# Which side of a raw page's round trip through memory is cut in four, and how many partitions each transfer spans

## The chip, the cores and the metric

The kernel runs on one core of a Trainium2 chip. The metric is the device time of one execution in microseconds (us). Engines are named as the profile names them: PE (TensorE), DVE (VectorE), ACT (ScalarE), POOL (GpSimd) and SP (SyncE). SP does no arithmetic here; its queue issues nearly all transfers, which 16 DMA engines then carry out.

## The reference

One transformer block with adaptive normalization, in float32, for `x` of 8 x 1024 x 512 and a condition of 8 x 512:

```
mod = silu(cond) @ Wada + bada            # six vectors of 512 for each sequence
sh_a, sc_a, gt_a, sh_m, sc_m, gt_m = split(mod, 6)
xm = layernorm(x, g1, be1) * (1 + sc_a) + sh_a
q, k, v = split(xm @ Wqkv, 3)             # 16 heads of 32
att = softmax(causal(q k^T / sqrt(32))) v
x = x + gt_a * (att @ Wproj + bproj)
xm = layernorm(x, g2, be2) * (1 + sc_m) + sh_m
x = x + gt_m * (gelu(xm @ W1 + b1) @ W2 + b2)   # hidden size 2048
```

## The kernel before, in words

The 8 sequences of 1024 tokens are cut into 16 blocks of 512 tokens. Each block goes through the normalization, the three projections, attention, the output projection and the two layers of the hidden part. The large products are done in Strassen's form, seven products of quarters in place of eight, with sums of weight quarters kept in memory. All weights pass through a ring of eight tiles `w` of 256 KB each (L358 to L362), fetched by SP in the order in which PE uses them; a tile is fetched anew when PE has used up the one in its place.

The order of all instructions on each engine is fixed when the program is built. A planner in the kernel keeps an estimated time for each engine and, for each buffer, when it is written and left (`now`, `written`, `left`; `note`, `note_pe`, `note_dma`). It chooses at each step the thread of work whose needs are due first. On the chip nothing is reordered: an engine that comes to an instruction whose operand is not there waits. In the built program each transfer of SP also waits for the landing of the transfer eight before it, since eight landing semaphores are used in turn.

Three places in it send data out to device memory and back, in order to change what lies in a partition.

The first is attention by rows. Six of the blocks (4, 6, 8, 10, 12 and 14) are attended "by rows": the scores of a unit have queries in partitions (`rows_unit`, L2017), ACT takes their exponential into a page `rows_p` of 128 x 2048 (L2036) and DVE transposes it in blocks of 32 x 32 (L2047). What is still to be moved are whole blocks between partitions. `spread_unit` does this by memory: it writes the page into `image` (L2060), gives its slot back, and later reads `image` into another page `turned` (L2076), from which PE forms the weighted values `po` (L2092). There are three page slots, and ten units in each of the six blocks, 60 in all. A read needs both the landed image and a free slot, and a slot becomes free when PE has used the page in it.

The second is the turn of normalized rows (`turn`): for 20 of the normalized tiles (14 for attention, 6 for the hidden part) the transposition is done by DVE in blocks (L714), one write of 1 MB into `held` (L723) and four reads into the tile `hat` (L728). DVE or ACT then apply gain and shift (L782, L788). The other tiles are transposed by PE (`by_pe`, L778).

The third is the load of `x` for the same 14 tiles of attention (`load_x`, L412): its token order in partitions has to be the one that the turn expects, so it is read in four transfers.

Q is 32 (`P // NTT`), NTT is 4, hd is 32, TB and D are 512. A transfer of 256 KB has 128 rows of 2 KB; as built before, each of the four `image` writes, `held` reads and `x` reads of one tile touches 32 partitions and has four rows for each of them.

Of the kernel before, what the change touches and what calls it, by code (L numbers as in the profile page):

```python
# [9 lines left out]
F32 = mybir.dt.float32  # L10
# [12 lines left out]
def kernel(  # L23
# [33 lines left out]
    nc = tc.nc  # L57
    B, T, D = x.shape
    HD = W1.shape[1]
    P = 128  # L60
    hd = D // H
    scale = float(hd) ** -0.5
    TB = 512
    NTT = TB // P
# [18 lines left out]
    kept = ctx.enter_context(tc.tile_pool(name="kept", bufs=1, space=bass.MemoryType.DRAM))  # L83
# [21 lines left out]
    def due(reads=(), writes=()):  # L105
        t = 0.0
        for k in reads:
            t = max(t, written.get(k, 0.0))
        for k in writes:
            t = max(t, left.get(k, 0.0))  # L110
        return t

    def note(engine, ns, reads=(), writes=(), port=False):
        start = max(now[engine], due(reads, writes))
        if port:
            start = max([start] + [b for a, b in pool_spans if a <= start < b])
        end = start + ns
        now[engine] = end
        if engine == "POOL":
            pool_spans.append((start, end))  # L120
            del pool_spans[:-16]
        for k in reads:
            left[k] = max(left.get(k, 0.0), end + SYNC)
        for k in writes:
            written[k] = end + SYNC
        return end

    def note_dma(ns, reads=(), writes=(), after=0.0):

        begun = max(now["SP"], due(reads, ()), after)  # L130
        now["SP"] = begun + ISSUE
        now["DMA"] = max(begun + BEGIN, now["DMA"]) + ns
        for k in writes:
            written[k] = now["DMA"] + LAND

    def note_pe(ns, form, reads=(), writes=()):
        now["PE"] = max(now["PE"], due(reads, writes))
        if shape[0] != form:
            shape[0] = form
            now["PE"] += SWITCH  # L140
        note("PE", ns, reads)
        spent[0] += ns
        for k in writes:
            written[k] = now["PE"] + PIPE
# [98 lines left out]
    def mlp_steps(n):  # L243
        return [("u", n, i) for i in range(NQ)] + [("d", n, part) for part in range(4)]
# [9 lines left out]
    for w in range(1, NB):  # L254
        n = w - 1
        m = mlp_steps(n)
# [29 lines left out]
    n = NB - 1  # L286
# [102 lines left out]
    rows = tmp.tile([P, TB], F32, tag="y", name="rows")[:n_rows, :P]  # L389
# [8 lines left out]
    Q = P // NTT  # L398

    def hat_tile(key):  # L400
        return tmp.tile([P, NTT, D], F32, tag="hat", name=f"hat_{key}", bufs=1)

    def load_x(n):
        b, h = blocks[n]
        rows = hat_tile(f"a{n}")
        written["hat free"] = NEVER
        for t in range(NTT):
            some = x[b, h * TB + t * P : h * TB + (t + 1) * P, :]
            if f"a{n}" in by_pe:
                nc.sync.dma_start(rows[:, t, :], some)  # L410
            else:
                nc.sync.dma_start(rows[ts(t, Q), :, :], some.rearrange("(t i) d -> i t d", i=Q))  # L412
            note_dma(3600, [], [("x", f"a{n}")])
        return rows

    x_pre = {0: load_x(0)}
    fetch()

# [134 lines left out]
    def add_job(job, reads, first=False):  # L553

        at = sum(1 for other in jobs if other[2]) if first else len(jobs)
        jobs.insert(at, (job, reads, first))
# [149 lines left out]
    def turn(key, rows, xm):  # L706

        small_blocks = xm.rearrange("p c n -> p (c n)")
        by_tile = small_blocks.rearrange("p (m h t i) -> p h m t i", m=NTT, h=NC, t=NTT)
        written["blocks", key] = NEVER  # L710

        def turn_tile(t):
            into = by_tile[:, :, :, t, :]
            nc.vector.transpose(into, rows[:, t, :].rearrange("p (h m i) -> p h m i", m=NTT, i=Q))  # L714
            done = [("blocks", key)] if t == NTT - 1 else []
            note("DVE", 620, [("hat", key, t)], done)

        for t in range(NTT):
            add_job(lambda t=t: turn_tile(t), [("hat", key, t)], key[0] == "m")
        yield [("blocks", key)], []  # L720
        held = kept.tile([P, NTT * D], F32, tag=f"held_{turns[0] % 2}", name=f"held_{key}")
        turns[0] += 1
        nc.sync.dma_start(held, small_blocks)  # L723
        note_dma(2600, [("blocks", key)], [("held", key)])
        yield [("held", key)], []
        for m in range(NTT):
            some = held[:, ts(m, D)].rearrange("(a i) d -> i a d", i=Q)
            nc.sync.dma_start(rows[ts(m, Q), :, :], some)  # L728
            note_dma(1250, [("held", key)], [("turned", key)])
        yield [("turned", key)], []  # L730

# [3 lines left out]
    def modulated(key, gain, shift, b, guards):  # L735
# [23 lines left out]
        if turned:  # L759
            yield from turn(key, got, xm)  # L760
# [590 lines left out]
    def perform(step):  # L1351
# [7 lines left out]
        elif kind == "columns_m":  # L1359
            columns_of["m"] = norm_columns("m", 3, 4, O_G2, O_BE2)  # L1360
        elif kind == "load_xa":
            x_pre[step[1]] = load_x(step[1])
        elif kind == "load_xr":
            start(load_xr(step[1]))
# [319 lines left out]
    def take_slot():  # L1684
        slot = free_p.pop(0)
        count_slots()
        return slot

    def give_slot(slot):
        free_p.append(slot)  # L1690
        count_slots()
# [362 lines left out]
    def spread_unit(n, raw, slot, parts, i):  # L2054

        yield [("p", slot)], []
        image = kept.tile([P, NTT, TB], F32, tag=f"image_{i % 5}", name=f"image_{n}_{i}")
        for a in range(NTT):
            into = image[:, a, :].rearrange("(b x) r -> x b r", x=hd)
            nc.sync.dma_start(into, raw[ts(a, hd)].rearrange("x (b r) -> x b r", b=NTT))  # L2060
            note_dma(700, [("p", slot)], [("image", n, i)])
        left["p", slot] = now["DMA"] + LAND
        written["image", n, i] += 1500
        raws.remove(slot)
        give_slot(slot)
        while True:
            yield [("image", n, i), SLOT, ("paged", n, i - 1)], []
            if free_p and len(pages) < 9:
                break
        taken_slot = take_slot()  # L2070
        pages.append(taken_slot)
        key = ("p", taken_slot)
        yield [], [key]
        written["paged", n, i] = 0.0
        page = pp.tile([P, NTT, TB], F32, tag=f"p{taken_slot}", name=f"turned_{n}_{i}")
        nc.sync.dma_start(page, image)  # L2076
        note_dma(2700, [("image", n, i)], [key])
        written[key] += 2000
        if i:
            yield [("valued rows", n, i - 1)], []  # L2080
        for qt, kh, c0, w, gg in parts:
            first = (n, gg) not in row_outs
            for k in range(w // P):
                yield [key, ("v", n), ("v done", n)], ["po"] if first and k == 0 else []
                if first and k == 0:
                    row_outs[n, gg] = [ps_po.tile([P, TB], F32, tag="o", name=f"po_{n}_{gg}"), 0]
                out = row_outs[n, gg]
                out[1] += 1
                for j in range(HPG):
                    r = slice(j * hd, (j + 1) * hd)  # L2090
                    at = c0 + k * P + j * hd
                    nc.tensor.matmul(  # L2092
                        out[0][r, ts(qt, P)],
                        vs[n][:, k, gg * P + j * hd : gg * P + (j + 1) * hd],
                        page[:, :, at : at + hd],
                        start=out[1] == 1,
                        stop=out[1] == 10,
                        skip_group_check=True,
                    )
                note_pe(2 * COLUMN * P, "columns", [key], ["po"])  # L2100
            if out[1] == 10:
                finish_rows(n, gg, out[0])
        pages.remove(taken_slot)
        give_slot(taken_slot)
        written["valued rows", n, i] = 0.0
# [27 lines left out]
    def finish_rows(n, g, out):  # L2133

        into = qTs[n][:, g, :]
        if wait_of(([("inverses", n, g)], [])) > 0 or max(now["DVE"], due(["po"])) > max(now["ACT"], due(["po"])) + 2500:
            nc.scalar.copy(into, out)
            note_act(585, None, ["po"], [("values", n, g)])
            start(scaled(n, g, into))
        else:  # L2140
            nc.vector.tensor_tensor(into, out, inverse_rows.pop((n, g)), ALU.mult)
            note("DVE", 690, ["po", "top"], [("att", n)])
            finished(n, g)
# [112 lines left out]
```

## Time and profile before

| | |
|---|---|
| median of 3 runs | 3537.45 us (3532.73 to 3537.84) |
| the profiled execution | 3537.05 us, span 3535.2 us |
| mean granted clock of TensorE | 0.988 |
| PE busy | 3398.7 us (96%) |
| DVE, ACT, POOL busy | 2287.1, 1249.8, 1790.1 us |
| moved | 610.88 MB, mean 173 GB/s |

The span is the time from the first to the last instruction of one profiled execution. A DMA queue's share is the time of its packets as a share of the span of all 16 DMA engines. In the rows of the profile a transfer is named by its tiles, as `turned<-image`, and SP's part of it, the issue, stands as SPq. TensorE works on float32 in two passes, so one matmul instruction has two records, and four matmuls of 32 columns run side by side.

### The profile page before, as it was taken

The numbers are of one execution on the slowest core, as the hardware profiler recorded it, in microseconds if no ns is written. First come the engines' busy times: TensorE is split into PE (matmuls) and PEld (weight loads), VectorE is DVE, ScalarE is ACT, GpSimd is POOL, SyncE is SP. The second block draws the span as 40 slices with busy tenths as digits, with TensorE's granted clock in tenths as the row PEclk, the third lists the DMA queues.
The fourth block names the chain that finished last, engine by engine and source line by source line (L and its number), as shares of the span: only waits on it lengthen the run. The fifth ranks groups of instructions, "written<-read, shape, count | busy, mean of one in ns | idle before, by whom it ended". The sixth has DMA issues, their size and how long they took to land.

```text
span 3535.2 us, 120275 instructions
## 1 busy us (share of the span) xinstructions
PE 3398.7 (96%) x53949; PEld 1726.5 (49%) x53949; DVE 2287.1 (65%) x2508; ACT 1249.8 (35%) x1878; POOL 1790.1 (51%) x1792
## 2 busy tenths in 40 slices
PE   8999999998999989999999999999999999999999
PEld 4444445454554545544454444544545445454455
DVE  5766675656667566675766657666667666576563
ACT  2334333252243522335323352323523334232421
POOL 3666846556038650476505764056730666308640
PEclk9999999999999999999999999999999999999999
DMA  6843434546755477553875548755487444863344
GB/s 199 262 149 112 139 94 137 149 113 209 231 187 155 115 236 222 182 152 109 262 234 166 146 116 266 235 159 145 134 280 219 140 141 159 276 200 110 96 134 140
DMA packets 373319, 610.88 MB, mean 173 GB/s; under 512 B 34748, under 2 KB 185084, under 8 KB 362308
## 3 DMA queue, kind: packets, MB, share of 16 engines
q1 hardware_dynamic: 372688, 603.15, 55.7%
q8 instruction: 425, 6.96, 0.8%
q14 instruction: 90, 0.74, 0.1%
q10 hardware_dynamic: 116, 0.03, 0.0%
HBM read 488.49 MB, written 112.46 MB: 170 GB/s over the span
## 4 chain that ended last, share of the span: by engine, by line
PE 78%; DVE 8%; DMA 6%; POOL 5%; issue 2%; SPq 1%; ACT 1%; ACTq 0%; DVEq 0%; POOLq 0%
PE bank L217 55%; PE sc L1613 6%; PE po L1760 5%; PE st L1719 5%; DMA turned<-image 3%; POOL pT L1854 3%; PE st L1707 2%; DVE mx L1628 2%; PE po L2092 2%; PE rows_sc L2017 1%; PE bank L1781 1%; DMA w<-in_L_cond_Wproj_dram 1%; DVE rows_max L2028 1%; DVE hT L167 1%; DVE sc L1625 1%
## 5 line engine op out<-in xcount | busy, mean ns | idle before, releaser
L1854 POOL TENSOR_TENSOR pT<-pT,pT 128x512 f32<-128x512 f32 (+3 forms) x966 | 1008.6, 1079 | 279.6 <-ACT pT L1732 230.1
L217 PE MATMUL bank<-w,hT 128*32 128x256 f32 x14336 | 824.3, 381 | 3.7 <-DVE hT L1226 2.9
L1732 ACT ACTIVATE pT<-st 128x2048 f32<-128x2048 f32 x228 | 428.3, 1879 | 749.5 <-PE st L1719 587.3
L1628 DVE TENSOR_REDUCE mx<-sc 128x4 f32<-128x2048 f32 (+3 forms) x287 | 522.8, 1839 | 243.0 <-PE sc L1613 239.6
L217 PEld LDWEIGHTS bank<-w,hT 128*32 128x32 f32 x14336 | 454.9, 110 | 388.0 <-issue 106.7
L217 PE MATMUL bank<-xm_m,w 128*32 128x256 f32 x8192 | 499.7, 381 | 0.0
L217 PE MATMUL bank<-t_m,w 128*32 128x256 f32 x6144 | 382.0, 380 | 8.2 <-DVE hT L208 8.2
L217 PEld LDWEIGHTS bank<-xm_m,w 128*32 128x32 f32 x8192 | 255.7, 110 | 218.5 <-issue 55.4
L2036 ACT ACTIVATE rows_p<-rows_sc,rows_minus 128x512 f32<-128x512 f32 (+3 forms) x384 | 196.8, 535 | 407.1 <-DVE rows_minus L2030 280.9
L217 PEld LDWEIGHTS bank<-t_m,w 128*32 128x32 f32 x6144 | 190.4, 110 | 181.9 <-issue 50.0
L1613 PE MATMUL sc<-kT,qT 32*128 32x512 f32 (+3 forms) x2296 | 262.1, 541 | 4.1 <-DVE mx L1628 2.4
L217 PE MATMUL bank<-w,qT 128*32 128x512 f32 x2048 | 245.1, 613 | 20.4 <-DMA w<-in_L_cond_Wproj_dram 19.5
L217 PE MATMUL bank<-xm_a,w 128*32 128x256 f32 x3968 | 245.8, 384 | 4.9 <-DVE u_q L208 2.2
L1760 PE MATMUL po<-pT,v 128*32 128x512 f32 (+3 forms) x2280 | 240.9, 513 | 7.1 <-POOL pT L1737 6.8
L1719 PE MATMUL st<-qT,kT 32*128 32x512 f32 (+3 forms) x2304 | 239.3, 505 | 0.0
L208 DVE TENSOR_TENSOR hT<-bank,u_u 128x512 f32<-128x512 f32 x183 | 122.7, 682 | 110.2 <-PE bank L217 102.5
L1737 POOL TENSOR_SCALAR_AFFINE_SELECT pT<-pT 128x512 f32<-128x512 f32 x160 | 117.9, 754 | 139.8 <-ACT pT L1732 139.8
L655 POOL TENSOR_SCALAR rstd_a<-mv_a 128x4 f32<-128x4 f32 x14 | 3.2, 230 | 363.2 <-DVE mv_a L634 362.8
L1625 DVE TENSOR_TENSOR sc<-sc,mask 128x1024 f32<-128x1024 f32 (+1 forms) x99 | 100.5, 1016 | 132.9 <-PE sc L1613 74.2
L217 PE MATMUL bank<-t_a,w 128*32 128x256 f32 x2944 | 185.3, 382 | 0.0
L217 PEld LDWEIGHTS bank<-xm_a,w 128*32 128x32 f32 x3968 | 127.6, 111 | 104.3 <-issue 23.0
L1129 ACT ACTIVATE hT<-hT,cols 128x512 f32<-128x512 f32 x256 | 164.8, 712 | 32.9 <-DVE hT L208 18.1
(270 smaller groups left out, 4149.7 us busy)
## 6 DMA issues: line engine op xcount, KB each, us to landing
w<-in_L_cond_W_dram SPq DMA_DIRECT2D x384, 256.0 KB
w<-kept_up_S SPq DMA_DIRECT2D x256, 256.0 KB
w<-kept_down_S SPq DMA_DIRECT2D x256, 256.0 KB
image<-rows_p SPq DMA_DIRECT2D x240, 256.0 KB
turned<-image SPq DMA_DIRECT2D x60, 1024.0 KB
w<-kept_qkv_S SPq DMA_DIRECT2D x180, 256.0 KB
w<-in_L_cond_Wqkv_dram SPq DMA_DIRECT2D x147, 256.0 KB
hat_a<-in_x_dram SPq DMA_DIRECT2D x64, 256.0 KB
```

The source lines that it names most:

```text
L208: nc.vector.tensor_tensor(out, src, other, op)
L217: nc.tensor.matmul(ps[r, :], columns, rhs, start=start, stop=stop, skip_group_check=True)
L1129: nc.scalar.activation(hT[:, i, :], hT[:, i, :], AF.Gelu, bias=cols[:, O_B1 + f : O_B1 + f + 1])
L1613: nc.tensor.matmul(sc[:, j, c0 : c0 + w], qTs[n][r, gg, ts(qt, P)], keys_of(n, kh)[r, gg, :w], start=True, stop=True, skip_group_check=True,)
L1625: nc.vector.tensor_tensor(place, place, shape_of.to_broadcast(place.shape), ALU.add)
L1628: nc.vector.tensor_reduce(maxima[n, gg][:, kh, qt, :], sc[:, :, c0 : c0 + w], axis=AX.X, op=ALU.max)
L1719: nc.tensor.matmul(st[:, j, c0 : c0 + w], kT[r, gg, ts(k % NTT, P)], qT[r, gg, TB - w :], start=False, stop=True, skip_group_check=True,)
L1732: nc.scalar.activation(pT[:, :, :used], st[:, :, :used], AF.Exp, scale=scale)
L1737: nc.gpsimd.affine_select(diagonal, diagonal, pattern=[[0, HPG], [1, P]], compare_op=ALU.is_ge, fill=0.0, base=0, channel_multiplier=-1,)
L1760: nc.tensor.matmul(po[r, TB - w :], v[:, k % NTT, g * P + j * hd : g * P + (j + 1) * hd], pT[:, j, c0 : c0 + w], start=(k == 0), stop=last ...
L1854: nc.gpsimd.tensor_tensor(into, into, pT[:, j, c0 : c0 + w], ALU.add)
L2036: nc.scalar.activation(tile_of[:, j], sc[:, j, c0 : c0 + w].rearrange("p (k b x) -> p k b x", b=NTT, x=hd), AF.Exp, bias=minus[:, i, j : j ...
```

## The change

For a unit's page the sides are exchanged: it is written by one transfer from all 128 partitions as it lies (8 KB rows), and read by four transfers, each of which fills one quarter of the length of all 128 partitions (2 KB rows). The reads of `held` and of `x` are still four for a tile, but each fills one quarter of all 128 partitions instead of the whole of 32. The bytes moved and the number of transfers stay as they are (1 + 4 in place of 4 + 1 for a unit). The planner's entries change with it: 2600 for the write in place of four times 700, and four times 690 for the read in place of 2700.

```diff
 load_x
-            some = x[b, h * TB + t * P : h * TB + (t + 1) * P, :]
             if f"a{n}" in by_pe:
-                nc.sync.dma_start(rows[:, t, :], some)
+                nc.sync.dma_start(rows[:, t, :], x[b, h * TB + t * P : h * TB + (t + 1) * P, :])
             else:
-                nc.sync.dma_start(rows[ts(t, Q), :, :], some.rearrange("(t i) d -> i t d", i=Q))
+                some = x[b, h * TB : (h + 1) * TB, :].rearrange("(m a i) d -> a m i d", a=NTT, i=Q)
+                nc.sync.dma_start(rows[:, t, :], some[t])
...
 turn
-        for m in range(NTT):
-            some = held[:, ts(m, D)].rearrange("(a i) d -> i a d", i=Q)
-            nc.sync.dma_start(rows[ts(m, Q), :, :], some)
+        for a in range(NTT):
+            some = held[ts(a, Q), :].rearrange("i (m d) -> m i d", m=NTT)
+            nc.sync.dma_start(rows[:, a, :], some)
             note_dma(1250, [("held", key)], [("turned", key)])
...
 spread_unit
-        image = kept.tile([P, NTT, TB], F32, tag=f"image_{i % 5}", name=f"image_{n}_{i}")
-        for a in range(NTT):
-            into = image[:, a, :].rearrange("(b x) r -> x b r", x=hd)
-            nc.sync.dma_start(into, raw[ts(a, hd)].rearrange("x (b r) -> x b r", b=NTT))
-            note_dma(700, [("p", slot)], [("image", n, i)])
+        image = kept.tile([P, NTT * TB], F32, tag=f"image_{i % 5}", name=f"image_{n}_{i}")
+        nc.sync.dma_start(image, raw)
+        note_dma(2600, [("p", slot)], [("image", n, i)])
...
-        nc.sync.dma_start(page, image)
-        note_dma(2700, [("image", n, i)], [key])
+        for a in range(NTT):
+            nc.sync.dma_start(page[:, a, :], image[ts(a, hd)].rearrange("x (b r) -> b x r", b=NTT))
+            note_dma(690, [("image", n, i)], [key])
```

## The prediction

> **What bounds the kernel now.** I read the page first: the parts on busy time, on the DMA queues and on the chain that ended last.
>
> ```profile
> span 3535.2 us, 120275 instructions
> PE 3398.7 (96%) x53949; PEld 1726.5 (49%) x53949; DVE 2287.1 (65%) x2508; ACT 1249.8 (35%) x1878; POOL 1790.1 (51%) x1792
> q1 hardware_dynamic: 372688, 603.15, 55.7%
> PE 78%; DVE 8%; DMA 6%; POOL 5%; issue 2%; SPq 1%; ACT 1%; ACTq 0%; DVEq 0%; POOLq 0%
> ```
>
> TensorE (PE) is busy for all but 3535.2 - 3398.7 = 137 us, so the change removes no work of the bounding engine; it can only alter how long PE waits. The DMA engines are busy 56% on average, but the kernel is uneven. So I asked next for the busy time of the six stretches in which a block is attended by rows, which is where the 60 raw pages go out to memory and come back. The first and the last of the six:
>
> ```profile
> core 0: us, PE busy (x) PEld busy (x) DVE busy (x) ACT busy (x) POOL busy (x), PEclk, DMA share, GB/s
> 833.00:1028.00 195.00, 176.28 (x2937) 96.04 (x2933) 134.56 (x160) 66.10 (x167) 33.01 (x34) 0.95 0.77 238
> 2977.00:3178.00 201.00, 191.56 (x3324) 106.97 (x3317) 140.64 (x158) 60.43 (x160) 46.52 (x37) 0.99 0.80 249
> ```
>
> In these 200 us stretches the DMA engines are already 0.77 to 0.80 busy, and PE idles 9 to 19 us in each. What PE waits for there stands in the list of waits (us in total, times, longest), and the chain shows one such wait in the fifth stretch (start, us, what).
>
> ```profile
> PEld po L2092 <- DMA turned<-image: 49.9, 19, 8.4
> PE po L2092 <- DMA turned<-image: 40.9, 18, 7.9
> ```
>
> ```profile
> 2613.03 1.05 PE po L2092 x32
> 2614.09 0.02 issue
> 2614.11 5.76 DMA turned<-image
> 2619.86 0.04 issue
> 2619.91 1.94 PE po L2092 x32
> ```
>
> When PE has used a page up, its slot is free, SyncE issues the next read into it at 2614.11, and PE stands still until it lands 5.8 us later. PE's order is fixed, so nothing is put in the gap. 19 + 18 = 37 waits on 60 reads: for most pages the read has no slack at all. A microsecond more per read is a microsecond more of time there.
>
> **How a transfer spreads.** The change keeps bytes and row lengths (8 KB rows one way, 2 KB the other) and changes which side is cut and how many partitions a transfer spans. I looked for moments in which one transfer ran nearly alone. First a 256 KB weight fetch into 128 partitions (317 to 318.7 us), then a 1 MB write of `held` from 128 partitions (1073.3 to 1077), a unit's writes from 32 partitions (3121 to 3127), and the 8 KB transfer of `inverse_rows` (883.9 to 885.2).
>
> ```profile
> DMA packets 144, 0.26 MB, mean 154 GB/s; under 512 B 16, under 2 KB 16, under 8 KB 144
> q1 hardware_dynamic: 144, 0.26, 42.4%
> ...
> DMA packets 144, 1.05 MB, mean 283 GB/s; under 512 B 16, under 2 KB 16, under 8 KB 16
> q1 hardware_dynamic: 144, 1.05, 69.1%
> ...
> DMA packets 681, 1.23 MB, mean 205 GB/s; under 512 B 80, under 2 KB 80, under 8 KB 681
> q1 hardware_dynamic: 681, 1.23, 93.3%
> ...
> DMA  0000000000000000000001222222000000000009
> DMA packets 69, 0.02 MB, mean 13 GB/s; under 512 B 68, under 2 KB 68, under 8 KB 68
> ```
>
> The first two have 128 data packets and 16 tiny ones, one with which each of the 16 DMA engines ends its part. The last has 64 packets of data (4 x 16 rows of 128 B) and only 4 tiny ones (the 69th packet is the next transfer's), and while it runs a fifth to a quarter of the DMA engines are busy (digit 2): its outermost dimension is 4, and 4 engines carried it. Costs in time of one engine: the weight fetch 0.424 x 16 x 1.7 us = 11.5 us, so 0.72 us on 16 engines or 2.9 us on 4. `held`: 0.691 x 16 x 3.7 = 40.9, 2.6 us on each of 16. The writes from 32 partitions: 0.933 x 16 x 6.0 = 89.6 us for 1.23 MB, which for 1.05 MB is 4.8 us on each of 16. So 32 partitions cost nearly twice what 128 do.
>
> The changed kernel's reads have, on the memory side, the list 4 x 32 x 512 (column block outermost), and on the SBUF side 128 x 512. No row of before mixes 4 and 128. The bounds are 4 engines and 16; I take 4, by the one row that has a 4 outermost. The Trainium skill, "DMA: Bandwidth & Descriptors", section on why a DMA increments its semaphore by 16, says that a transfer uses the largest number up to 16 that divides the slowest dimension of both sides; for 4 and 128 that is 4. The trace agrees for 4 with 4 (4 ending packets); for 4 with 128 no run here shows it.
>
> **The change part by part.** Durations are of the profiled execution, 3537.05 us around a span of 3535.2, which the median of the runs (3537.45) matches.
>
> Page reads (60, now four transfers each). One engine's part goes from 2.6 us (8 KB rows, taken from `held`) to 4 x 2.9 = 11.5 us: +8.9 us to landing. At the 37 waits nothing hides it: 329 us. The other 23 pages arrive before PE wants them, by how much differs: between 0 and 8.9 each; I take the middle, 102 us. What is late next is all that PE does behind `po`.
>
> Raw-page writes (60, now one transfer each): 4.8 to 2.6 us, -2.2. It counts where the read goes out as soon as the write lands:
>
> ```profile
> SPq L2076 <- DMA image<-rows_p: 9.9, 11, 1.8
> SPq L360 <- DMA turned<-image: 11.0, 5, 3.2
> ```
>
> 11 times: -24 us. Elsewhere the read waits for a slot and the gain is covered.
>
> SyncE's own time:
>
> ```profile
> L2060 SPq DMA_DIRECT2D image<-rows_p x240: 303/588/2450, 837.9 to 3157.4; - x120
> L2076 SPq DMA_DIRECT2D turned<-image x60: 319/374/1193, 846.7 to 3166.8; - x60
> L728 SPq DMA_DIRECT2D hat_a<-held_a x56: 302/430/1352, 137.1 to 3025.6; - x56
> ```
>
> 4 x 0.59 + 0.37 = 2.7 us per unit become 0.37 + 4 x 0.43 = 2.1 us. Nothing. Queued behind the reads on SyncE are the weight fetches.
>
> Normalized rows (20 turns of four reads): 4.8 us (32 partitions) become 11.5, +6.7. Who waited:
>
> ```profile
>   DVE xm_a L782: 10.6, 4
>   ACT xm_a L788: 9.1, 5
>   DVE xm_m L782: 2.9, 2
> ```
>
> 11 waits, of VectorE and ScalarE, not of PE. Behind them stand the evictions that free PE's three banks, so part of it comes through: between 0 and 20 x 6.7 = 134; I take half of 11 x 6.7, 37 us.
>
> Reads of `x` (14 blocks of four): nobody waits for them in the trace, they are early. But with the 20 turns they make 34 bursts that hold four engines 11.5 us instead of 4.8, and each weight fetch needs those four engines too. The cover is the ring of eight weight tiles:
>
> ```profile
> 2656.99 15.65 PE bank L217 x283
> PEld bank L217 <- DMA w<-in_L_cond_Wproj_dram: 24.8, 9, 6.4
> ```
>
> 283 records in 15.65 us are 55 ns each; a tile feeds 32 records, 1.8 us, and seven tiles in hand cover 12 us. That just hides a burst. Bounds 0 and 34 x 6.7 = 228; near the lower, 1 us each: 34 us.
>
> Waiting instructions of PE: as built, 969 instead of 866, since a page has four landings to wait for. At the one duration that the trace has for them, 103 x 0.051 = 5 us:
>
> ```profile
> L2092 PEldq EVENT_SEMAPHORE  x6: 51/51/51, 920.0 to 3080.8; - x6
> ```
>
> The sum: 329 + 102 - 24 + 37 + 34 + 5 = +483 us, 3537 + 483 = **4020 us**.
>
> A second way to it gives a floor. In a stretch of 201 us at 0.80, an engine works 161 us. For each of the four loaded engines: -10 x 2.6 (reads as they were) - 10 x 2.2 (writes) + 10 x 11.5 + 6.7 (one turn) = 235 us. Were they never idle, six stretches would grow by 6 x 34 = 204 us: 3741 us.
>
> **Rivals.**
> *Faster: the reads run on 16 engines.* What decides is which side's outermost dimension sets the spread; if it is the 128 of SBUF, a page read costs 4 x 0.72 = 2.9 us against 2.6, its fourth issue 3 x 0.43 = 1.3 us later, mostly under the moving data: +0.5 x 37 = +19. Writes -24, turns from 4.8 to 2.9 at 11 waits -21. Sum -26: 3511 us. For it: 32 partitions do cost twice here, and all three kinds of read now span 128. Against: the row with a 4. The Trainium skill, "SBUF — State Buffer", section on the DMA port swizzle, states this rule: 32 partitions reach 8 of the 16 ports, and only a transfer over all 128 reaches 16. The trace agrees (4.8 against 2.6 us). Chance 0.12.
> *Much slower: SyncE's queue backs up.* The row above in which a weight fetch (L360) waited for a page read, 5 times, shows that SyncE waits for unrelated earlier transfers; as built, a transfer waits for the landing of the one eight before it. If four slow reads hold half of these places, weights starve and every cover falls: 60 x 8.9 + 134 + 228 = 896, 4433 us. Chance 0.09.
> *Mildly slower: the planner's order covers the latency.* Then only the floor shows, 3741 us or a little less. Against: 37 waits without slack. Chance 0.07.
> That the change doesn't do what it says can be left out: as built there are 60 writes and 240 + 80 + 56 reads in the new form.
>
> **How the numbers follow.** Forecast 0.72, rivals 0.12, 0.09, 0.07. The forecast's own bounds are the floor, 3741, and all pages and turns at full price (534 + 134, with the 34 and the 5 and no gain at the writes), 4244. For 8 in 10 I reach into both slower rivals: 3700 to 4330 holds nearly all of 0.72, half of 0.09 and most of 0.07. The measurement of this kernel tells about 0.2% from no change. Faster by more: 0.08, same 0.02 (both from the first rival), slower 0.90.
>
> **What would show it.** Right: PE's wait for `turned` rises from 91 us to some 400; a page read in the chain takes 13 us and more instead of 5.8; around a read the DMA digits stand near 2 to 4 with only four tiny packets per transfer; the six stretches are 55 to 80 us longer, at a lower share. Wrong: sixteen tiny packets per read, or page reads that land in 5 to 7 us; then the time is near 3511. If the reads are slow and PE's waits are for `w` instead, it is the second rival.

## The result, and the profile after

The changed kernel takes 4108.79 us, the median of 4 runs (4100.91 to 4115.63), against 3536.19 us (3532.73 to 3537.84) before: a ratio of 1.162, 95% interval 1.1597 to 1.1643. It is 573 us slower; the forecast was 483.

The page of the profile after, the same rows as before: span, engines, the queue, the chain by engine and, after it, by line.

```profile
span 4099.1 us, 120422 instructions
PE 3509.1 (86%) x53949; PEld 1789.5 (44%) x53949; DVE 2337.2 (57%) x2537; ACT 1242.5 (30%) x1869; POOL 1810.4 (44%) x1778
DMA packets 368808, 610.87 MB, mean 149 GB/s; under 512 B 30236, under 2 KB 180572, under 8 KB 357796
q1 hardware_dynamic: 368176, 603.13, 46.0%
PE 59%; DMA 24%; DVE 7%; SPq 4%; POOL 4%; issue 2%; ACT 1%; ACTq 0%; DVEq 0%; POOLq 0%
PE bank L217 41%; DMA turned<-image 12%; PE sc L1613 5%; PE po L1760 4%; PE st L1719 4%; POOL pT L1854 3%; SPq L2075 2%; DMA hat_a<-held_a 2%; DMA image<-rows_p 2%; PE po L2091 2%; PE st L1707 1%; DMA w<-in_L_cond_Wproj_dram 1%; DVE mx L1628 1%; PE rows_sc L2017 1%; DMA hat_m<-held_m 1%
```

The span grew by 564 us. PE's idle time went from 137 us to 590 (4099.1 - 3509.1), +453, and its busy time by 110 us at the same count of matmuls. The bytes are the same. DMA's share of the chain went from 6% to 24%. The queue's packets are 4512 fewer (372688 - 368176): 376 reads in the new form, each with 12 ending packets less (4 in place of 16).

Where it went: the six stretches of attention by rows, which now take 1694 us together instead of 1191 (first, last and sum of the six; the sum of before below them; the last three columns are granted clock, DMA share, GB/s).

```profile
858.00:1133.00 275.00, 185.28 (x2888) 102.58 (x2884) 136.43 (x158) 64.21 (x166) 36.27 (x35) 0.83 0.51 167
3448.00:3740.00 292.00, 212.44 (x3344) 119.51 (x3340) 142.76 (x158) 60.31 (x161) 45.89 (x37) 0.85 0.53 172
sum 1694.00, PE 1214.09 PEld 677.84 DVE 864.21 ACT 385.06 POOL 281.66; mean PE 202.35 PEld 112.97 DVE 144.03 ACT 64.18 POOL 46.94
```

```profile
sum 1191.00, PE 1111.44 PEld 617.77 DVE 851.14 ACT 383.35 POOL 265.23; mean PE 185.24 PEld 102.96 DVE 141.86 ACT 63.89 POOL 44.21
```

So 503 of the 564 us lie there, 84 us a stretch, at a DMA share that *fell* from about 0.8 to about 0.5 with the same bytes to move. A mean over 16 engines is a poor gauge when 4 of them do the work: those four can be busy without a break while the mean looks relaxed. The view of one page read that ran nearly alone (1441 to 1454.2 us) shows it directly.

```profile
DMA  0201222222222222222222222222222222221000
GB/s 0 50 0 19 56 81 87 93 99 106 99 106 99 106 93 99 99 99 106 99 93 99 99 99 99 99 99 99 99 99 93 93 99 99 93 99 62 6 0 0
DMA packets 529, 1.07 MB, mean 81 GB/s; under 512 B 16, under 2 KB 16, under 8 KB 528
q1 hardware_dynamic: 528, 1.05, 21.4%
```

The DMA digit stands at 2 (a quarter of 16 engines is 0.25), and four transfers leave 16 ending packets, 4 each. 0.214 x 16 x 13.2 us = 45.2 us of engine time, 11.3 us on each of four; the prediction worked with 11.5. By the Trainium skill, "DMA: Bandwidth & Descriptors", section on why a DMA increments its semaphore by 16, lists that begin with 4 on one side and 128 on the other go to 4 engines, the largest number up to 16 that divides both; the trace now agrees.

What PE waited for, by the list of waits (us, times, longest) and by the view of the line of `po` alone (us, times), and the chain at three such reads (start, us, what):

```profile
PE po L2091 <- DMA turned<-image: 374.6, 50, 15.6
```

```profile
  DMA turned<-image: 422.1, 57
```

```profile
1440.95 0.54 SPq L2075
...
1442.66 11.23 DMA turned<-image
1453.88 0.25 issue
1454.13 1.97 PE po L2091 x32
...
1457.78 11.70 DMA turned<-image
1469.48 0.14 issue
1469.62 1.08 PE po L2091 x16
...
1475.58 13.24 DMA turned<-image
```

The view of the line adds two rows of the list, PE's 374.6 us and 47.5 us of its weight loads (PEld), and these are the same moments: each of the 7 waits of the weight loads ends within 0.1 us of one of PE's 50. So PE's own waits for pages went from 40.9 us in 18 waits (the row of before in the prediction) to 374.6 us in 50.

A cycle of the loop "slot free, issue, land, use" now takes 15 to 18 us (1440.95 to 1456.11, and from there to the next first issue at 1473.90). From the first issue to the landing pass 12.9, 13.4 and 14.9 us in these three reads; before, it was 5.76 us.

### The profile page after: what moved, and what is told of

It is laid out like the page before. It is cut to its first block, busy times and chain, and to the rows that moved or that the text cites. A ratio compares the mean times of both kernels' runs of the same rounds, so it can differ in the third digit from the quotient of the medians.

```text
span 4099.1 us, 120422 instructions
## 1 busy us (share of the span) xinstructions
PE 3509.1 (86%) x53949; PEld 1789.5 (44%) x53949; DVE 2337.2 (57%) x2537; ACT 1242.5 (30%) x1869; POOL 1810.4 (44%) x1778
## 3 DMA queue, kind: packets, MB, share of 16 engines
q1 hardware_dynamic: 368176, 603.13, 46.0%
## 4 chain that ended last, share of the span: by engine, by line
PE 59%; DMA 24%; DVE 7%; SPq 4%; POOL 4%; issue 2%; ACT 1%; ACTq 0%; DVEq 0%; POOLq 0%
PE bank L217 41%; DMA turned<-image 12%; PE sc L1613 5%; PE po L1760 4%; PE st L1719 4%; POOL pT L1854 3%; SPq L2075 2%; DMA hat_a<-held_a 2%; DMA image<-rows_p 2%; PE po L2091 2%; PE st L1707 1%; DMA w<-in_L_cond_Wproj_dram 1%; DVE mx L1628 1%; PE rows_sc L2017 1%; DMA hat_m<-held_m 1%
## 5 line engine op out<-in xcount | busy, mean ns | idle before, releaser
L217 PE MATMUL bank<-xm_m,w 128*32 128x256 f32 x8192 | 508.3, 386 | 3.5 <-DVE xm_m L782 3.5
L2091 PE MATMUL po<-turned,v 128*32 128x128 f32 x1920 | 111.3, 391 | 409.5 <-DMA turned<-image 374.6
L217 PE MATMUL bank<-xm_a,w 128*32 128x256 f32 x3968 | 258.1, 402 | 23.0 <-ACT u_k L204 13.3
L2091 PEld LDWEIGHTS po<-turned,v 128*32 128x32 f32 x1920 | 79.5, 154 | 453.2 <-issue 371.9
L217 PE MATMUL bank<-t_a,w 128*32 128x256 f32 x2944 | 195.8, 395 | 0.0
```

The costliest lines, as they stand in the source:

```text
L217: nc.tensor.matmul(ps[r, :], columns, rhs, start=start, stop=stop, skip_group_check=True)
L2091: nc.tensor.matmul(out[0][r, ts(qt, P)], vs[n][:, k, gg * P + j * hd : gg * P + (j + 1) * hd], page[:, :, at : at + hd], start=out[1] == 1 ...
```

## The experiments

Two theories stood at the start. *Four engines*: a read whose list in memory has a 4 outermost runs on four engines, and everything that waits for it, or queues behind it on those four, pays. *Another cause*: the width of 128 partitions, the row length, the order that the planner made of the new entries, or PE itself.

**The three parts one by one.** Each kernel has one hunk of the change alone: `spread_unit` (pages_only), `turn` (turns_only), `load_x` (x_only).

> Only the round trip of the units' pages is as changed; the reads of held and of x are as before. If four engines carry each page read (theory), 60 reads that take some 13 us and more instead of 6 bring most of the loss: 3960 to 4060 us. If the loss comes from all three kinds of read in proportion to their bytes (60 MB of pages, 20 of held, 14 of x), about 3540 + 573 x 60/94 = 3900 us.

> Only the 20 x 4 reads of held are as changed. Theory: VectorE and ScalarE wait about 6.7 us more at each, PE has other work meanwhile, so 37 us by the prediction's term, 3575 us; up to 134 us (3670) if each wait comes through whole. By bytes, as the rival of the run above has it: 3540 + 573 x 20/94 = 3660 us.

> Only the 14 x 4 reads of x are as changed. Nobody waits for them in the trace of before; theory: the weight fetches behind a burst on four engines lose about 1 us each, 14 us at most, 3537 to 3552 us. The changed kernel less the one with only the pages (4109 - 4025 = 84 us) and the one with only the turns (+87) leave about nothing for it. By bytes: 3540 + 573 x 14/94 = 3620 us.

| part alone | us | ratio, 95% interval | against before |
|---|---|---|---|
| pages_only | 4024.66 (4023.25 to 4025.41) | 1.1384 (1.1367 to 1.1401) | +488 |
| turns_only | 3623.35 (3616.22 to 3634.12) | 1.0252 (1.0228 to 1.0276) | +87 |
| x_only | 3541.12 (3533.06 to 3549.69) | 1.0013 (1.0002 to 1.0024) | +4 |

The three add up to 579, and together they cost 573: they hardly overlap. The pages are the bulk. `x` costs next to nothing, as expected. The turns cost more than twice their term. In the waits of turns_only VectorE and ScalarE now wait 94 us for their tiles (23 us before), and PE and its weight loads wait longer for the weights of the output projection (PE 48.7 us against 19.5). One of these waits, of 11.5 us, ended at 2673.9 us; SP had issued three of the weight fetches at 2660.9 us, right behind the four reads of a turn:

```profile
DVE xm_a L782 <- DMA hat_a<-held_a: 32.6, 4, 9.3
ACT xm_a L788 <- DMA hat_a<-held_a: 29.5, 6, 7.4
DVE xm_m L782 <- DMA hat_m<-held_m: 20.3, 3, 7.7
ACT xm_m L788 <- DMA hat_m<-held_m: 11.8, 3, 4.8
...
PEld bank L217 <- DMA w<-in_L_cond_Wproj_dram: 49.5, 10, 13.3
```

**The same split of work, without a 4 outermost.** pages_into_32 keeps the one write of a page from 128 partitions and the four reads, but each read fills 32 partitions, so that both lists begin with 32 (its edit against pages_only).

```diff
-        for a in range(NTT):
-            nc.sync.dma_start(page[:, a, :], image[ts(a, hd)].rearrange("x (b r) -> b x r", b=NTT))
+        for m in range(NTT):
+            some = image[:, ts(m, TB)].rearrange("(a x) r -> x a r", x=hd)
+            nc.sync.dma_start(page[ts(m, hd), :, :], some)
```

> The page is written by one transfer from 128 partitions, as in the changed kernel, and read by four, but each read fills 32 partitions whole, with lists of 32 x 4 x 512 on both sides. If the spread over DMA engines is what costs, the reads run on 16 engines at 4.8 us of moving instead of 11.5: some 2 to 3.5 us more than before at 37 waits, less the 24 us of the writes: 3590 to 3650 us. If what costs is that the side that PE waits for is cut in four (2 KB rows, four issues, four landings), this is no better than with the pages as changed: 3900 us or more.

3624.69 us (3613.6 to 3631.31), ratio 1.0252 (1.0223 to 1.0281): of the pages' 488 us, 400 are gone. The 89 that are left lie within 60 x 2.2 us, what 32 partitions cost above 128 by the rows of the prediction. In the profile PE's waits for pages are 57 us longer than before (97.7 against 40.9) and its work 28 us (3426.7 against 3398.7). The waits for pages:

```profile
PE po L2092 <- DMA turned<-image: 97.7, 39, 9.5
PEld po L2092 <- DMA turned<-image: 10.0, 5, 2.7
```

**The kernel before, with a 4 outermost.** page_list_of_4 changes only the shape of `image` in memory: one row of padding after each 32 keeps the single read of a page from being one flat list of 128 there; it becomes 4 x 32 x 2048. PE's order of instructions is that of the kernel before.

```diff
-        image = kept.tile([P, NTT, TB], F32, ...)
+        image = kept.tile([NTT, hd + 1, NTT, TB], F32, ...)
...
-            into = image[:, a, :].rearrange("(b x) r -> x b r", x=hd)
+            into = image[:, :hd, a, :].rearrange("b x r -> x b r")
...
-        nc.sync.dma_start(page, image)
+        nc.sync.dma_start(page.rearrange("p a r -> p (a r)"), image[:, :hd].rearrange("b x a r -> b x (a r)"))
```

> The kernel before in all but one thing: the image in memory has a gap after every 32 of its 128 rows, so that the one read of a page has a list of 4 x 32 x 2048 on the memory side. Writes, rows of 8 KB, number of transfers and PE's order are those of before. If an outermost dimension of 4 puts the read on four engines: 4 x 2.6 = 10.2 us of moving instead of 2.6, so 7.7 us at 37 waits and half of it at 23, 285 + 89, and what PE's clock loses in the waits: 3900 to 4000 us. If the cut on the read side is what costs, or the planner's other order: 3537 us, no change.

4224.97 us (4216.19 to 4231.42), ratio 1.195 (1.1925 to 1.1974). The direction was expected, the size (3900 to 4000) was not: this is slower than the whole change. A page read that ran alone (1448.1 to 1467 us):

```profile
DMA  0051212322231222213321231223122221100000
...
DMA packets 133, 1.06 MB, mean 56 GB/s; under 512 B 4, under 2 KB 4, under 8 KB 4
q1 hardware_dynamic: 132, 1.05, 20.1%
```

Four ending packets for one transfer, so four engines again; but 0.201 x 16 x 18.9 / 4 = 15.2 us on each, not 11.3. Two more runs asked why. page_list_of_4_short_rows pads the rows too (`[NTT, hd + 1, NTT, TB + 16]`), which makes 2 KB rows of the 8 KB ones; page_list_of_4_in_four reads that same image by four transfers of 256 KB (its edit against page_list_of_4_short_rows):

```diff
-        nc.sync.dma_start(page, image[:, :hd, :, :TB])
+        for a in range(NTT):
+            nc.sync.dma_start(page[:, a, :], image[:, :hd, a, :TB])
```

> The kernel before, with the image padded in memory so that the one read of a page has the list 4 x 32 x 4 x 512 there: 4 outermost as with page_list_of_4, but rows of 2 KB instead of 8 KB, 512 data packets instead of 128. If the length of the rows is what made page_list_of_4 slower than the changed kernel (15.2 us on each of four engines against 11.3), a page read alone takes about 11.3 us on each of four engines, and the time lies near that of pages_only: 3980 to 4080 us. If instead one instruction with four engines is dearer than four such instructions, whatever the rows, the time is 4200 to 4250 us, as with page_list_of_4.

> As page_list_of_4_short_rows, same image in memory and same 2 KB rows on the same four engines, but a page is read by four transfers of 256 KB, one for each quarter of the rows' length, instead of by one of 1 MB. In the changed kernel, also with four transfers, a page read took 11.3 us on each of four engines; as one transfer it took 16.5. If the size of one transfer is what makes the difference, a page takes 11 to 12 us here and the time is 3980 to 4080 us; if it is where the rows lie in memory, it takes about 16 us and the time stays at 4250 to 4330 us.

The short rows were no faster, and slower than either theory had it: 4287.83 us (4282.12 to 4306.56), ratio 1.2125 (1.2095 to 1.2156). Four transfers in place of one were faster, as the theory of one dear transfer had it: 4066.83 us (4061.93 to 4075.08), ratio 1.1502 (1.1474 to 1.1529). One page read of each, nearly alone (1455 to 1474 us of the first, 1406.9 to 1420.2 us of the second):

```profile
GB/s 0 0 52 26 56 73 73 60 60 73 60 47 47 82 69 52 52 78 86 52 56 73 73 69 65 78 60 86 78 69 65 95 69 43 43 47 43 13 13 4
...
q1 hardware_dynamic: 516, 1.05, 21.7%
```

```profile
GB/s 0 0 0 0 49 62 80 80 43 43 92 49 68 99 99 99 111 99 99 105 99 99 99 105 99 99 99 99 99 99 92 105 99 92 99 99 99 99 99 31
...
q1 hardware_dynamic: 528, 1.05, 22.4%
```

0.217 x 16 x 19 / 4 = 16.5 us against 0.224 x 16 x 13.3 / 4 = 11.9 us: the same rows and four engines in both, some 65 GB/s as one transfer and 99 as four. So neither the row length nor the place in memory makes the difference, but that the page goes as one transfer. Why is open; the second row also starts slowly and reaches 99 only after a few us, as does the changed kernel's.

The four kernels side by side: added time, the same over the added time of one read (above 2.6 us), and from the profiles PE's own waits for pages and what its work grew by (before: 40.9 us in 18 waits, 3398.7 us).

| kernel | a page read, us on each of 4 engines | added, us | added per us of read | PE's waits for pages, us (times) | PE's work, us more |
|---|---|---|---|---|---|
| pages_only | 11.3 (as in the changed kernel) | 488 | 56 | 372.0 (50) | 111 |
| page_list_of_4_in_four | 11.9 | 530 | 57 | 385.2 (48) | 108 |
| page_list_of_4 | 15.2 | 689 | 55 | 583.0 (55) | 114 |
| page_list_of_4_short_rows | 16.5 | 750 | 54 | 659.8 (55) | 114 |

There are 60 page reads, and 48 to 55 of them now stop PE. The time grows nearly in proportion to what a read got slower, but 54 to 57 is not a count of reads that bear their full price: in pages_only PE waits 331 us more for pages, 111 us are slower work of PE, and the rest of the 488 are other waits.

**PE's slower matmuls.** In the changed kernel `po` is slower per instruction (min/median/max in ns, before and after):

```profile
L2092 PE MATMUL po<-turned,v x1920: 269/273/423, 860.8 to 3174.4; 128*32 128x128 f32 x192
```

```profile
L2091 PE MATMUL po<-turned,v x1920: 272/421/424, 886.2 to 3737.4; 128*32 128x128 f32 x192
```

The granted clock, the share of TensorE's full speed that the profile records, fell within the first of the three waits shown above. The columns are as in the stretches, the clock is the third from the end: before the wait and, once the page had landed, at its `po`.

```profile
1442.00:1445.00 3.00, 2.32 (x24) 0.51 (x16) 2.97 (x4) 2.44 (x7) 0.00 (x0) 1.00 0.23 83
1454.00:1456.00 2.00, 1.87 (x36) 1.90 (x40) 0.00 (x0) 0.00 (x0) 0.00 (x0) 0.50 0.00 0
```

busy_in_waits gives PE eight groups of spare matmuls ahead of a unit's first `po`, in 54 places (54 x 8 x 4 = 1728 instructions, two records each); less_busy_in_waits gives it four groups.

```diff
                 out = row_outs[n, gg]
+                if (qt, kh, c0, w, gg) == parts[0] and k == 0 and bank_at() < NEVER:
+                    spare = lin_bank()
+                    for _ in range(8):
+                        for j in range(HPG):
+                            ...
+                            nc.tensor.matmul(banks[spare][r, :], vs[n][:, 0, r], vs[n][:, 0, :], ...)
+                    live[spare] = False
```

> The changed kernel, with eight groups of spare matmuls on PE (some 7 us, their result is not used) ahead of the first use of a page, 54 times, where PE stands still for a page 9 to 15 us. In the changed kernel PE's busy time rose by 110 us with the same instructions (a po matmul 273 to 421 ns). If that is the clock, which falls because PE stands idle, the spare work lies inside the waits, the granted clock in the six stretches rises from about 0.86 to 0.95, the po matmuls go back to some 300 ns, and the time falls to 4020 to 4080 us. If the slower matmuls come from the DMA traffic or from something else, they stay at 420 ns, and the time is 4109 us or, where the spare work doesn't fit into a wait, up to 4300.

> The changed kernel, with four groups of spare matmuls ahead of a unit's first po instead of eight (some 190 us of PE work in 54 places instead of 383; their result is used nowhere). If PE's slower clock is a part of the time, so much spare work fits into the waits almost whole, po matmuls get back towards 273 ns and the time falls by some 40 to 80 us: 4030 to 4070. If the arrival of the pages sets the end whatever PE does between, the time stays at 4100 to 4120 us, though PE's work on po gets shorter.

busy_in_waits: 4126.31 us (4121.74 to 4134.85), ratio 1.1666 (1.1648 to 1.1683). less_busy_in_waits: 4126.83 us (4116.46 to 4128.8), ratio 1.1655 (1.1632 to 1.1678). With eight groups the matmuls are fast again:

```profile
L2101 PE MATMUL po<-turned,v x1920: 269/273/423, 909.6 to 3757.1; 128*32 128x128 f32 x192
...
L2092 PE MATMUL bank<-v 128*32 128x512 f32 x3456 | 382.9, 595 | 21.8 <-POOL v L170 17.9 <-ACT xm_m L788 1.7 <-DVE y L208 1.4
```

So idle PE is what made them slow, as that theory said: the reads were as before, and the clock in the six stretches was 0.94 to 0.98 in place of 0.83 to 0.88. Its hope for the time (4020 to 4080 us) failed: 383 us of spare work cost 17 us in all, yet none came off. PE's busy time without the spare work fell by 81 us (3811.0 - 382.9 = 3428.1 against 3509.1), and 102 us of the spare work did not fit into the waits (idle time fell from 590 to 309 us, 281 of 383). The half dose could not settle it, since it left the median at 417 ns; its time, too, was not the 4030 to 4070 us hoped for. How much of the 110 us of slower PE work is on the path stays open.

**Can the round trip do without a cut?** Both remaining runs start from the kernel before. keys_by_four lets ACT read the scores in steps of four, so that a partition's keys lie as 4x + b; then the write and the read of a page are one plain transfer each with 128 outermost on both sides.

```diff
-    sc[:, j, c0 : c0 + w].rearrange("p (k b x) -> p k b x", b=NTT, x=hd),
+    sc[:, j, c0 : c0 + w].rearrange("p (k x b) -> p k b x", b=NTT, x=hd),
...
-            into = image[:, a, :].rearrange("(b x) r -> x b r", x=hd)
-            nc.sync.dma_start(into, raw[ts(a, hd)].rearrange("x (b r) -> x b r", b=NTT))
+        nc.sync.dma_start(image.rearrange("a (x b) r -> (a x) (b r)", b=NTT), raw)
...
-        nc.sync.dma_start(page, image)
+        nc.sync.dma_start(page, image.rearrange("a p r -> p a r"))
```

> The kernel before with another order of the keys in a page: the exponential reads each 128 keys as 32 x 4 in place of 4 x 32, so that after the transposition the key is 4 x + b, and both the write and the read of a page are single transfers of 128 partitions with lists of 128 on both sides. Theory: 16 engines and full width both ways, 2.6 us for the write (4.8 before) and 2.9 for the read (2.6 before), one issue each in place of five: 3490 to 3530 us, if reading PSUM with a step of four elements costs ScalarE little (its 384 exponentials take 535 ns each). If the step doubles that, 205 us of ScalarE, of which a part comes through: 3550 to 3700 us.

3534.36 us (3528.39 to 3543.39), ratio 0.9989 (0.9979 to 0.9999): short of the 3490 to 3530 us expected. ACT's reading in steps is free (686 ns for the widest form, as before), but PE's waits for pages hardly fall, from 40.9 us to 39.8 (those of the weight loads from 49.9 to 42.1):

```profile
L2036 ACT ACTIVATE rows_p<-rows_sc,rows_minus 128x512 f32<-128x512 f32 x96 | 64.7, 686 | 150.4 <-DVE rows_minus L2030 126.9 <-DVE rows_sum L2111 23.4
```

```profile
PEld po L2090 <- DMA turned<-image: 42.1, 20, 7.8
PE po L2090 <- DMA turned<-image: 39.8, 17, 7.3
```

keys_and_features_by_four does the same for the normalized rows: VectorE transposes the features 4i + m together, and a tile is read by one transfer of 1 MB into 128 partitions.

```diff
-    nc.vector.transpose(into, rows[:, t, :].rearrange("p (h m i) -> p h m i", m=NTT, i=Q))
+    nc.vector.transpose(into, rows[:, t, :].rearrange("p (h i m) -> p h m i", m=NTT, i=Q))
...
-            some = held[:, ts(m, D)].rearrange("(a i) d -> i a d", i=Q)
-            nc.sync.dma_start(rows[ts(m, Q), :, :], some)
+        nc.sync.dma_start(rows, held.rearrange("a p d -> p a d"))
```

> The run above, and the same idea for the turns: VectorE's transposition takes a row's features as 32 x 4 in place of 4 x 32, so that held is read by one transfer of 128 partitions and 2 KB rows in place of four of 32 partitions (2.9 us of moving instead of 4.8, one issue instead of four). Theory: a further 5 to 20 us less, 3475 to 3520 us. If VectorE reads slower with a step of four elements, 80 transpositions of 670 ns double: up to 54 us more.

3522.9 us (3516.51 to 3529.84), ratio 0.9957 (0.9944 to 0.997): faster than both kernels, by 0.4%, a little less than the 3475 to 3520 us expected. The weight loads' wait for the output projection's weights falls from 24.8 us to 4.9, while VectorE's transposes get dearer, 676 to 1128 ns, where VectorE has room (it is busy 65% of the span before). A wait of this kernel, then its transposes, then those of the kernel before:

```profile
PEld bank L217 <- DMA w<-in_L_cond_Wproj_dram: 4.9, 5, 1.5
```

```profile
L714 DVE STREAM_TRANSPOSE xm_a<-hat_a 128x512 f32<-128x512 f32 x56 | 60.9, 1128 | 0.0
```

```profile
L714 DVE STREAM_TRANSPOSE xm_a<-hat_a 128x512 f32<-128x512 f32 x56 | 35.7, 676 | 0.0
```

## Why the prediction was right, point by point

*What sets the spread.* Right, and it carried the rest: four engines, 11.3 us where 11.5 was said. The first rival (16 engines, 3511 us) is out by the 4 ending packets of each read. The runs show it from both sides: without the 4 most of the pages' cost goes, and a 4 alone in the kernel before brings 530 to 750 us.

*The page reads.* The term was 431 us; PE's waits for pages rose by 334. The mechanism held, but the term started from a misreading. The 37 waits without slack are 18 of PE and 19 of its weight loads, and most of these are the same moments (at 2619.91 us, for one, both have a wait). Nor did PE stand still for the whole 5.76 us there:

```profile
2613.86 3.62 PE L217 MATMUL bank<-w,qT 128*32 128x512 f32 x32
2619.91 1.94 PE L2092 MATMUL po<-turned,v 128*32 128x128 f32 x32 [2.43 <-DMA turned<-image]
```

It worked on the output projection for the first 3.6 us and waited for 2.4. So at most 18 reads of the 60 had no slack, not 37. With 18 at the full 8.9 us and 42 at half of it the term would have been 347 us, close to the 334 measured, and the whole sum 399. Reads that used to arrive in time by less than 9 us did lose their slack: 18 waits became 50. The 91 us that were to become some 400 are the same sum of two rows (422 now).

*The writes.* Taken as -24; this step failed. A write on 16 engines lands only when its last part does, and a quarter of it waits behind the read issued before it:

```profile
1599.43 14.04 DMA image<-rows_p
```

```profile
DMA  5558999999999989699984333223222421132201
```

SP had issued a page read at 1594 to 1596 us; the write behind it took 14 us. The second row is the DMA share from 1599.4 to 1613.5 us: in its second half it mostly stands at 1 to 4. Of the write's 128 packets of 8 KB, 96 had started 5.4 us after the issue and the last 32, four engines' worth, only between 9.7 and 13.3 us, about when that read had landed (PE's wait for it ended at 1609.8 us, 10.4 after the issue). All seven such writes in the chain have this gap between 96 and 32; in pages_into_32, with the same writes and no read of the pages on four engines, none of 59 has it (0.08 us at most). In the chain, such writes now hold 2%, 86 us; before they held 19. By the Trainium skill, "DMA: Bandwidth & Descriptors", in the section named above, a transfer that SP issues on k engines takes the lowest-numbered k. That all slow reads share the same four fits these packets, though no row names the engines.

*The turns.* Taken as 37, within bounds of 0 to 134; alone they cost 87. Half of 11 waits at 6.7 us was too little, and part of the price came where the 34 us for weights were entered: PE's waits for the output projection's weights went from 19.5 to 48.7 us. Of that entry `x` used 4 us. Both terms together were 71; both parts measured 91.

*PE.* The sum held PE's work constant; the change was to "only alter how long PE waits". PE's work grew by 110 us, 103 of them in the six stretches (1214.09 against 1111.44), with a granted clock of 0.83 and 0.85 in the two shown. This was not in the sum at all. What the sum did forecast, waits, came to 453 us more against 483. So that the forecast is 90 us off and no more is in part luck: the reads without slack were counted about twice, the writes were given a gain where they lost, and slower work was left out.

*SyncE.* No cost was entered, and the second rival said its queue would back up (4433 us). Some of that is seen in SP's waits, but it is small, and the time stayed 324 us below the rival:

```profile
SPq L2075 <- DMA turned<-image: 63.8, 18, 10.5
SPq L358 <- DMA turned<-image: 24.4, 16, 4.0
```

*The floor.* 3741 us by throughput was a floor and no forecast: each stretch grew by 84 us, not 34, and a little beyond the 55 to 80 that had been given. That fits a loop of slot, read and use that is bound by latency (the cycle of 15 to 18 us above), not by the load of four engines; no run tests this by itself.

## What to carry to other kernels

Before a transfer is reshaped, write out both lists and look at the outermost length of each: here a 4 on the memory side took 11 us and more for 1 MB that 16 engines move in 2.6, though the other side spanned all 128 partitions. If the data has to be cut in four, let the cut be an inner dimension, or choose the order of the elements at the compute step so that no cut is left (here that gave 0.4%). And when a read gets slower than the slack it has, expect nearly all reads of the loop to be waited for, not those alone that are today (18 became 50 of 60); count each wait once, for the matmuls or for their weight loads; and enter what the slower clock after each wait costs.

## What the runs showed of the hardware that was not expected

On four engines 1 MB as one transfer took 15.2 us on each (rows of 8 KB) and 16.5 (rows of 2 KB), as four transfers 11.3 and 11.9 (rows of 2 KB). The cause stays open.

A write on 16 engines that is issued behind a read on four took 14.0 us to land, because its last quarter waited.

A TensorE that waits some 10 us for a page runs its next matmuls at 421 ns instead of 273, with the granted clock at 0.50 in the row above, and eight groups of spare matmuls in the waits bring the 273 back (four left 417). The Trainium skill, "TensorE: Matmul & The Clock Gate", section "Part 1: The HAM clock gate", says that an idle window of about 3.4 us halves PE's clock and a busy one restores it; the trace agrees in kind (the granted clock fell from 1.00 to 0.50 in a wait of 9.8 us, and to 0.83 over the first stretch), and the forecast would have gained by entering it.

ScalarE reads scores from PSUM in steps of four elements at no cost (686 ns both ways); VectorE's transpose from SBUF in steps of four takes 1128 ns instead of 676.
